# Reordering VectorE and GpSimd work around the head statistics of a self-attention block

## The chip, the cores and the metric

The kernel runs on one core of a Trainium2 chip. The metric is the time of the launch on the device in microseconds (us). Three runs are shown, and their median is used. One more execution was taken by the hardware profiler, and all views of the profile come from it.

The engines of the core are named as in the profile: PE (TensorE, matrix products and transposes), PEld (its weight loads), DVE (VectorE), ACT (ScalarE), POOL (GpSimd) and SP (SyncE, which only issues transfers here). Each engine works through its own queue of instructions in order; between engines they wait on semaphores.

## The reference, cut to what matters

The program is two layers of a gated transformer over 16 batch items of 128 tokens and 256 features. The change touches only the first attention layer (the functions `_ln`, `_div_clamp_fp8` and `_gqa` of the reference):

```python
ln_out = _ln(hidden_states, ln_w, ln_b)
q = _fp8_linear_pertensor(ln_out, wq, wq_scale, q_in_scale).reshape(b, s, g, hpg, d)
q = _ln(q, qln_w, qln_b)
k = _fp8_linear_pertensor(ln_out, wk, wk_scale, k_in_scale).reshape(b, s, g, d)
k = _ln(k, kln_w, kln_b)
v = _fp8_linear_pertensor(ln_out, wv, wv_scale, v_in_scale).reshape(b, s, g, d)
core = _gqa(q, k, v).reshape(b, s, nh * d)          # self-attention, 16 heads, 8 groups, d = 128
qx = _fp8_linear_pertensor(ln_out, wqx, wqx_scale, qx_in_scale)  # cross-attention to the context
...
xout = _gqa(qx, kx, vx).reshape(b, s, nh * d)
catq = _div_clamp_fp8(jnp.concatenate([core, xout], axis=-1), proj_smooth)
return jnp.einsum('bsi,oi->bso', catq, wproj) * (proj_in_scale * proj_w_scale)
```

Here `_ln` normalises each head over its 128 features, `_fp8_linear_pertensor` divides its input by a scale per feature, clamps it, rounds it to 8-bit floating point and multiplies by a weight matrix, and `_gqa` is softmax attention in which two query heads share one key head. After this layer come a gated feed-forward layer, a second attention layer and a layer of eight experts; the change does not touch them.

## The kernel before

The first attention layer is 32 units of work (class `Unit`): one self-attention unit for each batch item (units 0 to 15), then one cross-attention unit for each (16 to 31). A unit takes four steps of the loop over `n` at the end of the class, and in each step several units are at different stages. In the loop, `do(n, lag, name)` calls a stage for one of a unit's four chunks of four heads, and `once(n, step, name)` calls a stage once for a unit.

The stages, in the order in which a self-attention unit meets them:

- `prep_norm`, `prep_tr`, `prep_scale`: the item's rows are normalised (DVE), transposed (PE) and divided by the scales of the four kinds of input, queries, keys, values and cross queries (POOL, tile `in_y`).
- `prep_round` and `prep_last`: rounding to 8 bits in `e4m3`. Four DVE operations (clamp, mask of the exponent, scaling it, an addition, lines 225 to 231) give the tiles `e_e` and `e_t`; POOL subtracts them (line 237). Before the change it writes two tiles, `xs` (queries, keys and values, 768 columns) and `xx` (cross queries, 256 columns). SP then stores `xx` in DRAM (line 409), from where the cross unit loads it 16 units later.
- `project` and `evict`: eight blocks of 512 columns, two for the keys, four for the queries, two for the values, as products on PE (line 431), copied to `raw` or `vt` by ACT (lines 443 and 440). `bn` takes the statistics of each head of `raw` on DVE (line 452).
- `rstd`: four small DVE operations on 24 columns (lines 459 to 464, `q_dif` and `q_var`) give the variances of the unit's 24 heads; `rsqrt0` gives their inverse roots: logarithm and exponential on ACT (lines 308 and 309), then one Newton step of three DVE operations (lines 310 to 312, `q_r`).
- `mult`: POOL scales four heads of `raw` by `q_r` (line 475, six times a unit). `heads`: PE transposes them (line 486), and ACT evicts them with weight and bias of the norm into `kT` or `qT` (line 495).
- `scores` (PE, line 504), `top` (the maximum, DVE, line 512), `exp` (ACT, line 520), `recip` (DVE, line 528), `divide` (POOL, line 532), `probs` (transposes on PE, line 540, evicted by ACT, line 542), `values` (PE, line 550), `smooth` (DVE, line 561).
- `quant` and `quant_last`: the same rounding for the attention's output; POOL writes `cat` (line 237). `output` multiplies by the projection (PE, line 591), and `residual` adds the result to the input (DVE, line 605).

In the step in which `rstd` of unit u runs, unit u-1 is at its chunk 2: its scores, maximum and exponentials come first in the loop. The same step has `prep_last` of unit u+1, the `mult` of the two key blocks and of the first query block of unit u, and `quant` of the last chunks of unit u-2. In the next step the keys of unit u+1 are projected, and the division of chunk 2 of unit u-1 comes.

The order on each engine is not the order of the program's text. A scheduler arranges the instructions of each engine when the kernel is built: an instruction that is ready by the scheduler's own estimate of times is placed, and among several ready ones that which comes first in the text. The queue that results is fixed, and on the chip each engine keeps to it. `stay_after(ins, other)` adds an edge for this arrangement: `ins` is put behind `other`. Both are on the same engine in all uses here, so it costs no wait. Before the change it is used only in `quant_last`, where the last write of `cat` is put behind the third scaling of the unit that is two ahead (`scaled`).

Tiles rotate: `raw` has nine buffers, most others two, `in_y` one. In PSUM the scores have two buffers, which the estimate in `rsqrt0` shares, and the values one.

Of the kernel before, what the change touches and what calls it, by code (L numbers as in the profile page):

```python
# [18 lines left out]
P = 128  # L19
B = 16  # L20
# [15 lines left out]
def flamingo_kernel(  # L36
# [182 lines left out]
    def e4m3(dsts, y, pool):  # L219


        n = y.shape[1]
        e = pool.tile([P, n], BF16, tag="e8_e", name="e8_e")
        t = pool.tile([P, n], BF16, tag="e8_t", name="e8_t")
        nc.vector.tensor_scalar(y, y, FP8_MAX, -FP8_MAX, ALU.min, ALU.max)
        nc.vector.tensor_scalar(
            e.bitcast(U16), y.bitcast(U16), 0x7F80, None, ALU.bitwise_and
        )

        nc.vector.tensor_scalar(e, e, 2.0**-6, 24.0, ALU.max, ALU.mult)  # L230
        nc.vector.tensor_tensor(t, y, e, ALU.add)  # L231

        def last(other=None):
            at = 0
            for dst in dsts:
                part = slice(at, at + dst.shape[1])
                ins = nc.gpsimd.tensor_tensor(dst, t[:, part], e[:, part], ALU.subtract)  # L237
                if other is not None:
                    stay_after(ins, other)
                at += dst.shape[1]  # L240

        return last
# [11 lines left out]
    with (  # L254
# [48 lines left out]
        def rsqrt0(v, n, tag):  # L303

            a = small.tile([P, n], F32, tag=f"{tag}_a", name=f"{tag}_a", bufs=2)
            r = small.tile([P, n], F32, tag=f"{tag}_r", name=f"{tag}_r", bufs=2)
            est = ps_sc([P, n])
            nc.scalar.activation(a, v, AF.Ln)
            nc.scalar.activation(est, a, AF.Exp, scale=-0.5)
            nc.vector.scalar_tensor_tensor(a, est, -0.5, v, ALU.mult, ALU.mult)  # L310
            nc.vector.tensor_tensor(a, est, a, ALU.mult)
            nc.vector.scalar_tensor_tensor(r, a, 1.5, est, ALU.add, ALU.mult)  # L312
            return r

        norms = {}

        def stats(g):
# [13 lines left out]
            rr = rsqrt0(v, 4, "x")  # L331
# [3 lines left out]
        class Unit:  # L335
# [61 lines left out]
            def prep_round(self):  # L397
                if self.cross:
                    return
                xs = ap.tile([P, 6 * P], F32R, tag="xs", name="xs")  # L400
                xx = ap.tile([P, KD * P], F32R, tag="xx", name="xx")
                self.last = e4m3([xs, xx], self.y.rearrange("p i t -> p (i t)"), ap)
                self.xs, self.xx = xs, xx

            def prep_last(self):
                if self.cross:
                    return
                self.last()
                nc.sync.dma_start(out=xqx[self.b], in_=self.xx.bitcast(F32))
                lhs = [  # L410
                    [self.xs[:, (2 * kind + k) * P : (2 * kind + k + 1) * P] for k in range(KD)]
                    for kind in range(3)
                ]
                self.q_lhs, self.k_lhs, self.v_lhs = lhs[K_Q], lhs[K_K], lhs[K_V]

# [38 lines left out]
            def rstd(self):  # L454
# [4 lines left out]
                nc.vector.tensor_tensor(dif, st[:, :, 1], st[:, :, 4], ALU.subtract)  # L459
# [4 lines left out]
                nc.vector.scalar_tensor_tensor(var, var, 1.0 / P, dif, ALU.mult, ALU.add)  # L464
                self.r = rsqrt0(var, 24, "q")
# [44 lines left out]
            def top(self, c):  # L510
                mx = small.tile([P, 4], F32, tag="mx", name="mx")
                nc.vector.tensor_reduce(mx, self.sc[c], AX.X, ALU.max, negate=True)  # L512
# [17 lines left out]
            def divide(self, c):  # L530
                e, sums = self.e[c]
                nc.gpsimd.tensor_tensor(  # L532
                    e, e, sums[:, :, None].to_broadcast([P, 4, P]), ALU.mult
                )

# [30 lines left out]
            def quant(self, c):  # L566
                if c % 2 == 0:
# [4 lines left out]
                    self.cy.rearrange("p h s -> p (h s)"), ap,  # L572
# [119 lines left out]
        for n in range(first, last + 1):  # L692
# [12 lines left out]
            do(n, 0, "top")  # L705
            do(n, 0, "exp")
            if ab[0]:
                ab[0][0].project(ab[0][1])
                ab[0][0].evict(ab[0][1])
            once(n, -6, "prep_last")  # L710
# [4 lines left out]
            once(n, -2, "rstd")  # L715
# [5 lines left out]
            do(n, 3, "quant")  # L721
# [13 lines left out]
            once(n, -7, "prep_round")  # L735
# [618 lines left out]
```

## Time and profile before

| | |
|---|---|
| median of three runs | 1501.8 us (1501.51, 1501.80, 1504.62) |
| the profiled execution's own time | 1503.01 us |
| its span from first to last instruction | 1501.3 us |
| busy share PE, PEld, DVE, ACT, POOL | 91%, 64%, 66%, 56%, 46% |
| mean granted PE clock | 0.966 of full |
| instructions | 21652 |
| PE busy from 40 to 440 us (self-attention) | 361.23 of 400 us |
| PE busy from 440 to 870 us (cross-attention) | 415.93 of 430 us |

The page gives averages over stages with different limits, so the shares alone say little. Lines of the trace name an engine, a line of the program, an operation, the tiles written and read (`out<-in`), and the shape. In the timeline the first two numbers are the start and the duration in us, and the bracket gives how long the engine stood idle before, and what it then waited for. Where several instructions of one kind follow each other, they are one row (x3), and the duration is that of the row. Self-attention blocks in the steady part last 26.5 us, or 27.5 to 28 us in some of them.

### The profile page before, as it was taken

To read this page: it belongs to the slowest core of one execution; us is meant where nothing else is said; L and a number is where in the kernel's file an instruction comes from. 1 tells how busy PE (TensorE), PEld (TensorE's weight loads), DVE (VectorE), ACT (ScalarE), POOL (GpSimd) and SP (SyncE) were. 2 spreads that over 40 slices of the span, in tenths; PEclk is the share of its full clock that TensorE was granted. 3 is DMA by queue.
4 is the path that set the end of the run, shared out by engine and by line. 5 is a ranking of instruction groups with operands and counts; after the bars stand their busy time and mean duration, and the time that the engine had idled before them with its cause. 6 is when DMAs were issued, how large, how long until landed. Compare 5 with 4: busy or idle time off the path is not lost. (4 is left out here: it accounts for less than half of the span.)

```text
span 1501.3 us, 21652 instructions
## 1 busy us (share of the span) xinstructions
PE 1369.6 (91%) x6852; PEld 964.4 (64%) x6852; DVE 988.6 (66%) x2597; ACT 838.4 (56%) x2496; POOL 687.6 (46%) x615
## 2 busy tenths in 40 slices
PE   2789899899988999999999997999999999985998
PEld 1578778687776777777777766555544444444887
DVE  7867878778689777777676764453478787762100
ACT  3666566666656676666666663164476575741221
POOL 4476677677766565656556563121032322111111
PEclk9699999999999999999999998899999999986999
DMA  4300101000013100000000000700042212122652
GB/s 133 110 17 23 38 22 38 21 22 27 22 55 104 45 29 19 15 16 17 12 18 15 15 4 27 211 8 14 31 128 53 75 50 63 40 75 76 196 189 70
DMA packets 78770, 80.37 MB, mean 54 GB/s; under 512 B 15291, under 2 KB 64891, under 8 KB 78656
## 3 DMA queue, kind: packets, MB, share of 16 engines
q1 hardware_dynamic: 65152, 55.29, 12.7%
q10 hardware_dynamic: 11456, 17.63, 3.6%
q0 software_dynamic: 2048, 6.07, 1.1%
q8 instruction: 55, 0.90, 0.3%
q14 instruction: 59, 0.48, 0.1%
HBM read 57.14 MB, written 22.05 MB: 53 GB/s over the span
## 5 line engine op out<-in xcount | busy, mean ns | idle before, releaser
L532 POOL TENSOR_TENSOR e<-e,sums 128x512 f32<-128x512 f32 x128 | 141.4, 1105 | 239.7 <-DVE sums L528 100.8
L475 POOL TENSOR_TENSOR raw<-raw,q_r 128x512 f32<-128x512 f32 x192 | 211.3, 1126 | 21.0 <-DVE q_r L312 19.6
L520 ACT ACTIVATE e<-ps_sc,mx 128x128 f32<-128x128 f32 x512 | 181.1, 368 | 63.6 <-DVE mx L512 58.1
L452 DVE BATCH_NORM_STATS2 q_st<-raw 128x6 f32<-128x128 f32 x768 | 174.2, 279 | 64.2 <-ACT raw L443 63.6
L591 PE MATMUL ps_acc<-wp,cat 128*128 128x512 f32 x512 | 159.3, 433 | 14.0 <-POOL cat L237 13.4
L504 PE MATMUL ps_sc<-kT,qT 128*128 128x128 f32 x1024 | 140.9, 281 | 23.9 <-ACT qT L495 23.9
L542 ACT COPY eT<-ps_tr 128x512 f32<-128x512 f32 x128 | 75.3, 588 | 156.3 <-PE ps_tr L540 156.3
L504 PEld LDWEIGHTS ps_sc<-kT,qT 128*128 128x128 f32 x1024 | 132.4, 194 | 44.1 <-ACT qT L495 36.6
L237 POOL TENSOR_TENSOR cat<-e_t,e_e 128x1024 fp32r<-128x1024 bf16 x64 | 136.6, 2135 | 43.5 <-DVE e_t L231 43.5
L1082 ACT ACTIVATE e<-ps_sc,mx 128x128 f32<-128x128 f32 x512 | 139.0, 392 | 30.5 <-DVE mx L1073 30.1
L550 PE MATMUL ps_pv<-eT,vt 128*128 128x256 f32 x512 | 133.8, 383 | 1.0 <-DVE cat_y L561 1.0
L443 ACT COPY raw<-ps_mm 128x512 f32<-128x512 f32 x192 | 113.8, 593 | 29.2 <-PE ps_mm L431 25.8
L591 PEld LDWEIGHTS ps_acc<-wp,cat 128*128 128x128 f32 x512 | 94.6, 191 | 53.4 <-POOL cat L237 20.1
L486 PE MATMUL ps_tr<-ident,raw 128*128 128x128 f32 x768 | 115.2, 276 | 13.6 <-POOL raw L475 11.6
L486 PEld LDWEIGHTS ps_tr<-ident,raw 128*128 128x128 f32 x768 | 91.6, 141 | 47.5 <-POOL raw L475 20.5
L561 DVE TENSOR_TENSOR cat_y<-ps_pv,r_sm 128x512 bf16<-128x512 f32 x128 | 87.1, 680 | 47.2 <-PE ps_pv L550 46.7
L550 PEld LDWEIGHTS ps_pv<-eT,vt 128*128 128x128 f32 x512 | 97.3, 192 | 30.9 <-issue 10.5
L512 DVE TENSOR_REDUCE mx<-ps_sc 128x4 f32<-128x512 f32 x128 | 87.2, 682 | 38.5 <-PE ps_sc L504 37.8
L495 ACT ACTIVATE qT<-ps_tr,hv 128x512 f32<-128x512 f32 x128 | 101.2, 791 | 19.9 <-PE ps_tr L486 17.7
L520 ACT ACTIVATION_READ_ACCUMULATOR e<-ps_sc,mx 128x1 f32 x512 | 105.4, 206 | 0.0
L1093 PEld LDWEIGHTS ps_tr<-ident,e 128*128 128x128 f32 x512 | 59.9, 142 | 64.9 <-ACT e L1082 28.1
L1073 DVE TENSOR_REDUCE mx<-ps_sc 128x8 f32<-128x1024 f32 x64 | 77.6, 1212 | 30.2 <-PE ps_sc L1066 20.9
(221 smaller groups left out, 2687.0 us busy)
## 6 DMA issues: line engine op xcount, KB each, us to landing
w1t<-in_w ACTq DMA_DIRECT2D x8, 1024.0 KB
w2t<-in_w ACTq DMA_DIRECT2D x8, 1024.0 KB
disp<-empty SPq DMA_DIRECT2D x16, 257.0 KB
xe<-disp SPq DMA_DIRECT2D x8, 514.0 KB
ctx<-in_ctxT SPq DMA_DIRECT2D x32, 128.0 KB
stage<-in_wprojT SPq DMA_DIRECT2D x16, 256.0 KB
ods<-og SPq DMA_DIRECT2D x128, 32.0 KB
ov<-ods SPq DMA_DIRECT2D x32, 128.0 KB
```

What stands on the lines that cost most here:

```text
L237: ins = nc.gpsimd.tensor_tensor(dst, t[:, part], e[:, part], ALU.subtract)
L443: nc.scalar.copy(raw.rearrange("p h d -> p (h d)"), pm)
L452: nc.vector.bn_stats(self.st[:, 4 * blk + j, :], self.raws[blk][:, j, :])
L475: ins = nc.gpsimd.tensor_tensor(src, src, self.r[:, 4 * blk : 4 * blk + 4, None].to_broadcast([P, 4, P]), ALU.mult,)
L486: nc.tensor.transpose(pt[:, j, :], src[:, j, :], ident)
L495: nc.scalar.activation(dst, pt, AF.Identity, scale=hv[:, col : col + 1], bias=hv[:, col + 1 : col + 2])
L504: nc.tensor.matmul(pscore[:, j, :], qT[:, j, :], self.kT[:, 2 * c + j // 2, :], start=True, stop=True,)
L520: nc.scalar.activation(e[:, j, :], pscore[:, j, :], AF.Exp, bias=self.mx[:, j : j + 1], accum_out=sums[:, j : j + 1],)
L532: nc.gpsimd.tensor_tensor(e, e, sums[:, :, None].to_broadcast([P, 4, P]), ALU.mult)
L550: nc.tensor.matmul(pv[:, 2 * g : 2 * g + 2, :], self.vt[:, gg * P : (gg + 1) * P], eT[:, 2 * g : 2 * g + 2, :], start=True, stop=True,)
L591: nc.tensor.matmul(self.acc, self.cat[c // 2][:, h % 8, :], wpr[self.cross, c][:, j, :, :], start=(h == 0), stop=(h == 15),)
L1082: nc.scalar.activation(e[:, i, :], s[:, i // NQ, i % NQ, :], AF.Exp, bias=mx[:, i : i + 1])
```

## The change

Four things are changed, all in the first attention layer.

1. On DVE, in the step of `rstd`: first the maximum of the scores (`top`), then the variances (`rstd`, moved up in the text, its first operation put behind the maximum), then the rounding of the next unit's inputs (`prep_round`, moved from the end of the step before to this step; its clamp is put behind the last operation of the variances, or behind the maximum where there are no variances). The clamp of `quant` in this step is put behind the last operation of the Newton step.
2. The rounded inputs are four tiles of 256 columns instead of two of 768 and 256. `prep_last` now writes only that of the keys.
3. `prep_rest` is new: POOL writes the tiles of the queries, values and cross queries, behind the third scaling of the unit before, and SP stores the cross queries' tile after that.
4. The division of chunk 2 of a self-attention unit is put behind the third scaling of the unit after it.

```diff
@@ -216,13 +216,15 @@
             mean[:, :, None].to_broadcast([P, nh, P]), ALU.subtract,
         )
 
-    def e4m3(dsts, y, pool):
+    def e4m3(dsts, y, pool, behind=None):
 
 
         n = y.shape[1]
         e = pool.tile([P, n], BF16, tag="e8_e", name="e8_e")
         t = pool.tile([P, n], BF16, tag="e8_t", name="e8_t")
-        nc.vector.tensor_scalar(y, y, FP8_MAX, -FP8_MAX, ALU.min, ALU.max)
+        ins = nc.vector.tensor_scalar(y, y, FP8_MAX, -FP8_MAX, ALU.min, ALU.max)
+        if behind is not None:
+            stay_after(ins, behind)
         nc.vector.tensor_scalar(
             e.bitcast(U16), y.bitcast(U16), 0x7F80, None, ALU.bitwise_and
         )
@@ -230,14 +232,13 @@
         nc.vector.tensor_scalar(e, e, 2.0**-6, 24.0, ALU.max, ALU.mult)
         nc.vector.tensor_tensor(t, y, e, ALU.add)
 
-        def last(other=None):
-            at = 0
-            for dst in dsts:
-                part = slice(at, at + dst.shape[1])
-                ins = nc.gpsimd.tensor_tensor(dst, t[:, part], e[:, part], ALU.subtract)
+        def last(other=None, which=range(len(dsts))):
+            for i in which:
+                at = sum(d.shape[1] for d in dsts[:i])
+                part = slice(at, at + dsts[i].shape[1])
+                ins = nc.gpsimd.tensor_tensor(dsts[i], t[:, part], e[:, part], ALU.subtract)
                 if other is not None:
                     stay_after(ins, other)
-                at += dst.shape[1]
 
         return last
 
@@ -309,9 +310,11 @@
             nc.scalar.activation(est, a, AF.Exp, scale=-0.5)
             nc.vector.scalar_tensor_tensor(a, est, -0.5, v, ALU.mult, ALU.mult)
             nc.vector.tensor_tensor(a, est, a, ALU.mult)
-            nc.vector.scalar_tensor_tensor(r, a, 1.5, est, ALU.add, ALU.mult)
-            return r
-
+            return r, nc.vector.scalar_tensor_tensor(r, a, 1.5, est, ALU.add, ALU.mult)
+
+        tops = {}
+        vars_ = {}
+        rstds = {}
         norms = {}
 
         def stats(g):
@@ -328,7 +331,7 @@
 
             v = small.tile([P, 4], F32, tag="v1", name="v1", bufs=1)
             nc.vector.tensor_scalar(v, mv[:, :, 1], 1.0 + EPS, EPS * EPS, ALU.mult, ALU.add)
-            rr = rsqrt0(v, 4, "x")
+            rr, _ = rsqrt0(v, 4, "x")
             for j in range(4):
                 norms[4 * g + j] = (xg[:, j, :], mv[:, j, 0:1], rr[:, j : j + 1])
 
@@ -394,24 +397,35 @@
                 )
                 self.y = y
 
-            def prep_round(self):
+            def prep_round(self, n):
                 if self.cross:
                     return
-                xs = ap.tile([P, 6 * P], F32R, tag="xs", name="xs")
-                xx = ap.tile([P, KD * P], F32R, tag="xx", name="xx")
-                self.last = e4m3([xs, xx], self.y.rearrange("p i t -> p (i t)"), ap)
-                self.xs, self.xx = xs, xx
+                kinds = [
+                    ap.tile([P, KD * P], F32R, tag=f"x{slot}", name=f"x{slot}")
+                    for slot in ("qs", "ks", "vs", "x")
+                ]
+                self.last = e4m3(
+                    kinds, self.y.rearrange("p i t -> p (i t)"), ap, vars_.get(n, tops.get(n))
+                )
+                self.xs, self.xx = kinds[:3], kinds[3]
 
             def prep_last(self):
                 if self.cross:
                     return
-                self.last()
-                nc.sync.dma_start(out=xqx[self.b], in_=self.xx.bitcast(F32))
+                self.last(which=[K_K])
                 lhs = [
-                    [self.xs[:, (2 * kind + k) * P : (2 * kind + k + 1) * P] for k in range(KD)]
+                    [self.xs[kind][:, k * P : (k + 1) * P] for k in range(KD)]
                     for kind in range(3)
                 ]
                 self.q_lhs, self.k_lhs, self.v_lhs = lhs[K_Q], lhs[K_K], lhs[K_V]
+
+            def prep_rest(self):
+
+                if self.cross:
+                    return
+                u = units.index(self) - 1
+                self.last(units[u].scaled if u >= 0 else None, [K_Q, K_V, 3])
+                nc.sync.dma_start(out=xqx[self.b], in_=self.xx.bitcast(F32))
 
 
             def project(self, blk):
@@ -451,18 +465,22 @@
                 for j in range(4):
                     nc.vector.bn_stats(self.st[:, 4 * blk + j, :], self.raws[blk][:, j, :])
 
-            def rstd(self):
+            def rstd(self, n):
 
                 st = self.st
                 var = small.tile([P, 24], F32, tag="q_var", name="q_var", bufs=1)
                 dif = small.tile([P, 24], F32, tag="q_dif", name="q_dif", bufs=1)
-                nc.vector.tensor_tensor(dif, st[:, :, 1], st[:, :, 4], ALU.subtract)
+                ins = nc.vector.tensor_tensor(dif, st[:, :, 1], st[:, :, 4], ALU.subtract)
+                if n in tops:
+                    stay_after(ins, tops[n])
                 nc.vector.scalar_tensor_tensor(dif, dif, 0.25, dif, ALU.mult, ALU.mult)
                 nc.vector.scalar_tensor_tensor(
                     var, st[:, :, 2], P * EPS, st[:, :, 5], ALU.add, ALU.add
                 )
-                nc.vector.scalar_tensor_tensor(var, var, 1.0 / P, dif, ALU.mult, ALU.add)
-                self.r = rsqrt0(var, 24, "q")
+                vars_[n] = nc.vector.scalar_tensor_tensor(
+                    var, var, 1.0 / P, dif, ALU.mult, ALU.add
+                )
+                self.r, rstds[n] = rsqrt0(var, 24, "q")
 
             def mult_q(self, c):
                 self.mult(c + 2)
@@ -507,9 +525,9 @@
                     )
                 self.sc[c] = pscore
 
-            def top(self, c):
+            def top(self, c, n):
                 mx = small.tile([P, 4], F32, tag="mx", name="mx")
-                nc.vector.tensor_reduce(mx, self.sc[c], AX.X, ALU.max, negate=True)
+                tops[n] = nc.vector.tensor_reduce(mx, self.sc[c], AX.X, ALU.max, negate=True)
                 self.mx = mx
 
             def exp(self, c):
@@ -529,9 +547,12 @@
 
             def divide(self, c):
                 e, sums = self.e[c]
-                nc.gpsimd.tensor_tensor(
+                ins = nc.gpsimd.tensor_tensor(
                     e, e, sums[:, :, None].to_broadcast([P, 4, P]), ALU.mult
                 )
+                u = units.index(self) + 1
+                if c == 2 and u < B:
+                    stay_after(ins, units[u].scaled)
 
             def probs(self, c):
                 e, _ = self.e.pop(c)
@@ -563,13 +584,13 @@
                     r_sm[:, h0 : h0 + 4, None].to_broadcast([P, 4, P]), ALU.mult,
                 )
 
-            def quant(self, c):
+            def quant(self, c, n):
                 if c % 2 == 0:
                     return
                 cat = ap.tile([P, 8, P], F32R, tag="cat", name="cat")
                 self.clast = e4m3(
                     [cat.rearrange("p h s -> p (h s)")],
-                    self.cy.rearrange("p h s -> p (h s)"), ap,
+                    self.cy.rearrange("p h s -> p (h s)"), ap, rstds.get(n),
                 )
                 self.cat[c // 2] = cat
 
@@ -702,23 +723,25 @@
             do(n, 1, "divide")
             do(n, 0, "scores")
             do(n, 2, "probs")
-            do(n, 0, "top")
+            do(n, 0, "top", n)
             do(n, 0, "exp")
             if ab[0]:
                 ab[0][0].project(ab[0][1])
                 ab[0][0].evict(ab[0][1])
+            once(n, -2, "rstd", n)
+            once(n, -6, "prep_round", n)
             once(n, -6, "prep_last")
             do(n, 3, "values")
             do(n, 3, "smooth")
             if ab[0]:
                 ab[0][0].bn(ab[0][1])
-            once(n, -2, "rstd")
             for blk in range(2):
                 once(n, -2, "mult", blk)
                 once(n, -1, "heads", blk)
             do(n, -2, "mult_q")
             do(n, -1, "heads_q")
-            do(n, 3, "quant")
+            once(n, -6, "prep_rest")
+            do(n, 3, "quant", n)
             if ab[1]:
                 ab[1][0].project(ab[1][1])
                 ab[1][0].evict(ab[1][1])
@@ -732,7 +755,6 @@
             once(n, -8, "prep_norm")
             once(n, -8, "prep_tr")
             once(n, -7, "prep_scale")
-            once(n, -7, "prep_round")
 
     G = 4
     NT = G * P
```

## The prediction

> **What bounds the kernel now.** I read the page's first two parts first. TensorE (PE) is busy in 91% of the span, so the kernel can only gain where PE stands idle, or where its work shrinks; the change touches no PE work. Then I cut the span into stretches and compared a steady self-attention block with a steady cross-attention block (columns: stretch, us, then busy us and instructions for PE, PE's weight loads, VectorE, ScalarE, GpSimd, then granted clock):
>
> ```profile
> PE 1369.6 (91%) x6852; PEld 964.4 (64%) x6852; DVE 988.6 (66%) x2597; ACT 838.4 (56%) x2496; POOL 687.6 (46%) x615
> ...
> 310.00:336.50 26.50, 24.70 (x148) 20.76 (x147) 20.00 (x61) 17.11 (x54) 19.01 (x16) 1.00 0.08 23
> ...
> 600.00:626.50 26.50, 26.32 (x138) 19.64 (x137) 19.22 (x56) 17.12 (x53) 15.39 (x12) 1.00 0.05 15
> ```
>
> The clock is full in both. The cross block leaves PE 0.18 us idle, the self block 1.80 us of 26.50. Next, who PE waits for between 50 and 440 us (total, times, longest):
>
> ```profile
> PE ps_sc L504 <- ACT qT L495: 18.5, 12, 1.7
> PE ps_tr L486 <- POOL raw L475: 10.9, 21, 2.0
> ...
> PE ps_mm L431 <- DVE q_dif L459: 1.1, 1, 1.1
> ```
>
> Twelve blocks lose 1.46 to 1.69 us each at the scores, and 0.34 to 1.4 us at the transposes of the scaled heads. Last, the timeline of one such block shows why:
>
> ```profile
> 316.91 1.65 POOL L237 TENSOR_TENSOR xs<-e_t,e_e 128x768 fp32r<-128x768 bf16 x1 [0.63 <-DVE e_t L231]
> 317.36 1.26 DVE L459 TENSOR_TENSOR q_dif<-q_st 128x24 f32<-128x24 f32 x1
> ...
> 319.68 0.17 DVE L464 SCALAR_TENSOR_TENSOR q_var<-q_var,q_dif 128x24 f32<-128x24 f32 x1
> ...
> 319.89 0.22 ACT L308 ACTIVATE q_a<-q_var 128x24 f32<-128x24 f32 x1 [0.85 <-DVE q_var L464]
> 320.02 0.76 ACT L495 ACTIVATE qT<-ps_tr,hv 128x512 f32<-128x512 f32 x1
> ...
> 320.83 1.16 PE L504 MATMUL ps_sc<-kT,qT 128*128 128x128 f32 x8 [1.46 <-ACT qT L495]
> ...
> 322.27 3.03 POOL L475 TENSOR_TENSOR raw<-raw,q_r 128x512 f32<-128x512 f32 x3
> ...
> 324.36 0.66 PE L486 MATMUL ps_tr<-ident,raw 128*128 128x128 f32 x4 [0.34 <-POOL raw L475]
> ...
> 325.26 2.13 POOL L237 TENSOR_TENSOR cat<-e_t,e_e 128x1024 fp32r<-128x1024 bf16 x1
> ```
>
> A 24-column subtraction (q_dif, median 0.20 us over the kernel) takes 1.26 us and ends 0.06 us after GpSimd's write of xs. The logarithm on ScalarE waits for its result, the eviction of qT is queued behind the logarithm, and PE's scores wait for qT. The scaling of the heads then starts at 322.27, and PE meets it at 324.36. I use this block's times below.
>
> **What the change removes.** VectorE now takes the maximum, then the variances, then the rounding of the inputs. The scores end at 314.14. With the last 0.86 us of statistics ahead of it, the maximum (0.68) ends at 315.7, where it ended at 317.44. The variances' four operations (0.20, 0.17, 0.19, 0.17, some overlapped: 0.7) end near 316.4, not 319.85; GpSimd has no xs to write then. The exponentials on ScalarE (four at a pitch of 0.345) run 315.7 to 317.2, the value copy 0.6, logarithm 0.22, qT 0.76: qT is ready by 318.6. PE comes free for the scores at 318.89, after the transposes that start at 318.53. So the 1.46 us wait goes. Exponential and Newton steps follow, so q_r is ready near 319.4 instead of 321.93, and the heads' wait goes if GpSimd keeps up. Summed: scores 18.5; heads' waits in the same twelve blocks 10.9 less 2.35 (the block near 105 us) and 0.34 (near 80) = 8.2; the block near 100 us, 1.05 + 2.35 = 3.4. That is 30.1 us over 13 blocks, and no more is to be had in them.
>
> **What it adds and moves.** The rounding's four VectorE operations (0.43, 0.42, 0.43, 0.75, with a smoothing of 0.68 likely between) start at 316.4 and end near 319.05. GpSimd then writes the keys' inputs. The row for a 256-column write is 0.67 us (xx), so 319.75. The keys' projection can start when the scores leave PE, 318.89 + 0.9 = 319.8: no wait, with 0.05 us to spare. If q_r comes first and one scaling is ahead, 1 us.
>
> Behind it on GpSimd stand three scalings, then queries', values' and cross inputs (3 x 0.67), then cat (2.13), then the division of chunk 2 (1.04), which is now held behind the scalings as well. The input writes come to 4 x 0.67 = 2.68 us instead of 1.65 + 0.67 = 2.32. The DMA of the cross inputs moves with its write; SP's queue has nothing behind it that PE reads, and the data is read back sixteen blocks later. The rounding of cat is held behind the Newton steps on VectorE, so its four operations now lie beside the scalings, as they do in a cross block:
>
> ```profile
> 627.72 6.00 POOL L475 TENSOR_TENSOR raw<-raw,q_r 128x512 f32<-128x512 f32 x5
> ...
> 628.05 1.14 DVE L226 TENSOR_SCALAR e_e<-cat_y 128x1024 uint16<-128x1024 uint16 x1
> 629.23 1.15 DVE L230 TENSOR_SCALAR e_e<-e_e 128x1024 bf16<-128x1024 bf16 x1
> 630.41 1.41 DVE L231 TENSOR_TENSOR e_t<-cat_y,e_e 128x1024 bf16<-128x1024 bf16 x1
> ```
>
> There five scalings took 6.00 us, against 1.03 each alone: 0.17 us more apiece, and the VectorE operations 1.14 to 1.41 instead of about 0.43 to 0.69. The Trainium skill ("SBUF — State Buffer", section "Who interferes with whom") has a rule that speaks against this placing: a VectorE operation in a two-port mode, or with two SBUF inputs, and a GpSimd operation exclude each other, and whoever issues second is blocked for the other's whole instruction. By the rule three scalings could each lose a whole VectorE operation, 0.43 to 0.69, some 1.5 us a block; by the row they lose 0.5. I take the row. With the rule the gain would be 13 us smaller.
>
> So GpSimd: keys' inputs to 319.75, scalings at a pitch of 1.2 to 323.3, the rest to 325.4, cat to 327.5, division to 328.6. The heads' transposes (PE there about 1.5 us earlier than before, 321.9) need the first two scalings at 320.95 and 322.15: I charge 0.3 us a block, bounds 0 and 0.7. The projection with cat began at 327.45 and, 1.8 us earlier, would begin at 325.65: cat is 1.85 us late for it. PE has the next scores (0.9), a query projection (1.0) and values (0.9) to put first, if its queue is ordered so; the transposes that wait for the division (329.38 before, 327.6 then) can also stand behind these. Bounds 0 (all covered) and 1.85 plus something at the division; I take a third, 0.6. Together 0.9 x 13 = 11.7 us given back.
>
> Costed at nothing: in the 16 cross blocks the maximum goes ahead of the subtraction (623.90 and 623.78 now, 0.1 us), and cat's rounding already followed the Newton steps (627.47, 627.59). If the smoothing slips behind those steps, its cover is the next values, 5 us later (632.57); without it, 0.6 us a block. The boundary at 440 to 475 us, with 2.43 and 3.32 us waits, may shift by 2 us either way; I take 0. At the start, unit 0's rounding is issued after half of the queries' weights: between -1.4 us (0.67 instead of 2.08 before PE's first projection at 26.54) and +6; PE then waits 3.10 us for weights at 38.61, which covers most. I take 0. Unit 1's rounding now comes after unit 0's variances, which ended at 51.85, while its xs write ended at 50.6: K inputs up to 54.6 with 2.0 + 0.67, 4 us later, less what the variances gain (1.6 us of L460 was spent beside that write). I take +1.5, bounds 0 and 4.
>
> **Sum**: -30.1 + 11.7 + 1.5 = -16.9 against the profiled execution's own 1503.0 (span 1501.3): 1486.1. The median of the runs is 1.2 lower: 1485.
>
> **Rivals.**
> - *All of it is gained.* PE saturates as in the cross blocks (0.18 us idle): -30 + 1.5, 1473. For it: PE has other work at each late place. Against: GpSimd's queue is longer and nearer. Chance 0.2.
> - *GpSimd becomes the bound (slower).* One mechanism: cat stands behind the three input writes, and PE's queue keeps the projection where it was. Break-even is cat ending at 327.45, the old start. There a block lasts what it does now, and each further tenth of a us costs 1.3 us over 13 blocks. If scalings and writes lose what the rule says (1.0 more), cat ends at 328.5, 1.05 past that point: +13.7 us, less a third for blocks where PE has other work, so +9 on 1501.8, near 1510. For it: my cat time is 327.5, on the edge. Against: PE's weight loads wait little for cat now (0.8 us in 12 blocks), and 2.8 us of other PE work is at hand. Chance 0.22.
> - *The wait changes its name.* stay_after orders one engine; PE's queue had one keys' matmul ahead of the scores, at 318.89. If all four stay there, PE waits for the keys' inputs until 319.75 and the scores start at 320.8, as before; only heads' waits go, about 0.3 us a block: 1498, between 1494 and 1503. Chance 0.13.
> - *The forecast*, 1485, between 1477 and 1496: 0.45.
>
> **How the numbers follow.** A measurement of this kernel tells about 0.2% (3 us) from no change, so faster means under 1498.8 and slower over 1504.8. Faster: forecast and full gain 0.65, and a third of the renamed wait, 0.04: 0.69. Same: the rest of it near 1500, 0.06. Slower: 0.25, of which 0.22 the GpSimd case. The range 1472 to 1507 leaves out a little of the full gain and the further part of the slower case, together under 0.2.
>
> **What would show it.** Right: in the timeline q_dif takes 0.2 us and comes after the maximum and before in_y's clamp; the wait of L504 for qT falls from 18.5 to under 3 us; scalings start about 2.5 us earlier relative to the scores; self blocks last 25.0 to 25.6 us. Wrong: PE's waits list shows L591 for cat, L540 for e or L431 for the keys' inputs with more than 1 us a block, or blocks of 26.5 us and more; or the first 82 us have grown by more than 4.

## The result: 3.4% slower, and the profile after

The changed kernel takes 1555.1 us (median of 4 runs, 1550.1 to 1556.0); the kernel before took 1501.7 on the same chip. The ratio on record is 1.0335, with a 95% interval of 1.0313 to 1.0357 (the two medians alone give 1.0355). The profiled execution took 1555.4 us with a span of 1553.7, so 52.4 us more than the span before.

The first part of the page after, PE's row:

```profile
PE 1386.7 (89%) x6852; PEld 981.2 (63%) x6852; DVE 992.4 (64%) x2597; ACT 839.5 (54%) x2496; POOL 701.5 (45%) x647
```

PE runs the same 6852 instructions, yet is busy 17.1 us longer, and its share fell from 91% to 89%. Two things must have happened: new idle time, and slower work. The waits of PE between 50 and 440 us of the kernel after (total, times, longest) give the first:

```profile
PE ps_acc L612 <- POOL cat L239: 41.3, 12, 6.4
PE ps_tr L504 <- ACT kT L513: 7.1, 9, 0.8
PE ps_mm L445 <- POOL xks L239: 3.3, 3, 1.9
PE ps_tr L504 <- POOL raw L493: 3.2, 5, 2.1
```

The wait of the scores for qT, 18.5 us before, is off the list, and the wait for scaled heads fell from 10.9 to 3.2. A wait that was nowhere near the top before, that of the output projection (L612) for cat, stands at 41.3 us. Before, cat was ready only just in time: its write ended at 327.39 in the block of the prediction, and the projection began at 327.45 without a wait:

```profile
327.45 1.20 PE L591 MATMUL ps_acc<-wp,cat 128*128 128x512 f32 x4
```

The stretches of the kernel after give the second. The columns are those of the prediction's second fence; the first row is a whole self-attention block, the second the 6 us that begin 0.5 us before the projection starts:

```profile
317.70:347.70 30.00, 26.18 (x148) 22.11 (x147) 22.36 (x65) 17.24 (x56) 19.84 (x17) 0.94 0.07 20
...
328.00:334.00 6.00, 5.52 (x23) 4.91 (x24) 1.27 (x2) 2.13 (x10) 3.47 (x4) 0.72 0.01 3
```

The block has the 148 PE instructions that it had before, and lasts 30.00 us instead of 26.50. PE is busy 26.18 us instead of 24.70: 1.48 us more for the same work. Behind the wait the granted clock is 0.72 over 6 us; from 334 us to 347 us, in the rest of the block, it is 1.00 again. PE's timeline in this block shows both at the place:

```profile
324.82 0.66 PE L665 MATMUL ps_mm<-av,ctx 128*128 128x64 f32 x4
...
328.48 1.20 PE L612 MATMUL ps_acc<-wp,cat 128*128 128x512 f32 x4 [3.00 <-POOL cat L239]
329.51 1.46 PE L522 MATMUL ps_sc<-kT,qT 128*128 128x128 f32 x8
...
331.48 2.05 PE L445 MATMUL ps_mm<-wq,xqs 128*128 128x512 f32 x4
```

The last matmuls of kv1 (L661 and L665, products of the context that a later layer reads) end at 325.48, the projection starts at 328.48. The scores behind it take 1.46 us, where those at full clock take 1.05 to 1.16, and a query projection 2.05, where it took 1.18 before. Who wrote cat, and when, is in GpSimd's timeline of the same block:

```profile
317.81 0.67 POOL L239 TENSOR_TENSOR xks<-e_t,e_e 128x256 fp32r<-128x256 bf16 x1 [3.58 <-DVE e_t L233]
318.44 3.58 POOL L493 TENSOR_TENSOR raw<-raw,q_r 128x512 f32<-128x512 f32 x3
321.99 1.11 POOL L239 TENSOR_TENSOR xqs<-e_t,e_e 128x256 fp32r<-128x256 bf16 x1
323.06 0.67 POOL L239 TENSOR_TENSOR xvs<-e_t,e_e 128x256 fp32r<-128x256 bf16 x1
323.69 0.67 POOL L239 TENSOR_TENSOR xx<-e_t,e_e 128x256 fp32r<-128x256 bf16 x1
324.32 1.04 POOL L550 TENSOR_TENSOR e<-e,sums 128x512 f32<-128x512 f32 x1
325.32 1.03 POOL L493 TENSOR_TENSOR raw<-raw,q_r 128x512 f32<-128x512 f32 x1
326.32 2.11 POOL L239 TENSOR_TENSOR cat<-e_t,e_e 128x1024 fp32r<-128x1024 bf16 x1
```

VectorE's part of cat's rounding (e_t) ends at 322.57 and the third scaling at 322.02:

```profile
321.16 1.41 DVE L233 TENSOR_TENSOR e_t<-cat_y,e_e 128x1024 bf16<-128x1024 bf16 x1
```

GpSimd then runs three input writes, a division and a fourth scaling, and takes cat only at 326.32. The engine is not idle from 317.8 until cat is written, but its order is not PE's: what PE needs next is at the end of the row.

In two of the twelve blocks the scheduler put three scalings there instead of one. From GpSimd's and PE's timelines at that place:

```profile
292.63 3.03 POOL L493 TENSOR_TENSOR raw<-raw,q_r 128x512 f32<-128x512 f32 x3
295.62 2.11 POOL L239 TENSOR_TENSOR cat<-e_t,e_e 128x1024 fp32r<-128x1024 bf16 x1
...
297.79 2.07 PE L612 MATMUL ps_acc<-wp,cat 128*128 128x512 f32 x4 [6.38 <-POOL cat L239]
```

The projection alone then takes 2.07 us, where it takes 1.1 to 1.2 at the full clock. In the 6 us from 297.80 the granted clock is 0.59.

**Where the 52.4 us are.** I timed the blocks by the start of kv1 (L640 before, L661 after), which comes once a block. The first of the marks used stands at 108.93 before and 107.36 after, the mark twelve blocks later at 434.10 and 474.86. So the part ahead of the marks is 1.6 us shorter, and the twelve blocks are 42.3 us longer: 27.1 us each before and 30.6 after. The last 11.6 us come at the passage to cross-attention and in its first units; from 860 us (after: 912 us) on the distance stays. The stretches between the marks, before and after, in the columns of above, and PE's wait for cat in the second:

```profile
108.93:434.10 325.17, 298.23 (x1754) 249.60 (x1753) 251.20 (x744) 205.70 (x652) 225.74 (x181) 1.00 0.09 29
...
107.36:474.86 367.50, 315.30 (x1754) 266.15 (x1753) 252.09 (x743) 206.15 (x653) 237.89 (x205) 0.93 0.08 24
...
PE ps_acc L612 <- POOL cat L239: 42.8, 12, 6.4
```

At the same 1754 instructions PE is busy 17.1 us longer, at a granted clock of 0.93 instead of 1.00. Its idle time has grown by 25.3 us: 42.8 for cat (ten waits of 3.0 us, two of 6.4) and 8.3 for kT come in, the 18.5 for qT and some 8 for the heads go.

### The profile page after: what moved, and what is told of

Same layout as the page of the kernel before. It is cut to its first block, busy times and chain, and to the rows that moved or that the text cites. A ratio compares the mean times of both kernels' runs of the same rounds, so it can differ in the third digit from the quotient of the medians.

```text
span 1553.7 us, 21692 instructions
## 1 busy us (share of the span) xinstructions
PE 1386.7 (89%) x6852; PEld 981.2 (63%) x6852; DVE 992.4 (64%) x2597; ACT 839.5 (54%) x2496; POOL 701.5 (45%) x647
## 5 line engine op out<-in xcount | busy, mean ns | idle before, releaser
L550 POOL TENSOR_TENSOR e<-e,sums 128x512 f32<-128x512 f32 x128 | 136.3, 1065 | 245.2 <-ACT raw L457 131.2
L493 POOL TENSOR_TENSOR raw<-raw,q_r 128x512 f32<-128x512 f32 x192 | 220.8, 1173 | 12.8 <-DVE q_r L313 11.4
L612 PE MATMUL ps_acc<-wp,cat 128*128 128x512 f32 x512 | 166.2, 449 | 64.7 <-POOL cat L239 62.9
L612 PEld LDWEIGHTS ps_acc<-wp,cat 128*128 128x128 f32 x512 | 98.0, 198 | 107.0 <-POOL cat L239 70.8
L522 PEld LDWEIGHTS ps_sc<-kT,qT 128*128 128x128 f32 x1024 | 141.6, 205 | 23.3 <-ACT qT L513 14.4
L522 PE MATMUL ps_sc<-kT,qT 128*128 128x128 f32 x1024 | 148.8, 292 | 2.5 <-ACT qT L513 2.5
L504 PEld LDWEIGHTS ps_tr<-ident,raw 128*128 128x128 f32 x768 | 92.9, 143 | 52.6 <-issue 27.1
```

The lines of the kernel that those rows point to most:

```text
L493: ins = nc.gpsimd.tensor_tensor(src, src, self.r[:, 4 * blk : 4 * blk + 4, None].to_broadcast([P, 4, P]), ALU.mult,)
L504: nc.tensor.transpose(pt[:, j, :], src[:, j, :], ident)
L522: nc.tensor.matmul(pscore[:, j, :], qT[:, j, :], self.kT[:, 2 * c + j // 2, :], start=True, stop=True,)
L550: ins = nc.gpsimd.tensor_tensor(e, e, sums[:, :, None].to_broadcast([P, 4, P]), ALU.mult)
L612: nc.tensor.matmul(self.acc, self.cat[c // 2][:, h % 8, :], wpr[self.cross, c][:, j, :, :], start=(h == 0), stop=(h == 15),)
```

## The experiments

Unless said otherwise a diff is against the kernel after, the ratio is to the kernel before on the same chip (medians 1501.1, 1502.2 and 1503.7 in the three groups) with its 95% interval, and a block's length is taken between kv1 marks; where one figure is given, it is that of most blocks. In the expectations, theory A says that cat is late because of what stands ahead of it in GpSimd's queue while PE's queue keeps the projection where it is.

**1. Cat ahead of the three input writes (e1_cat_first).** The write of cat is kept as `wrote`; the input writes, the division and the later scalings are held behind it. Everything that the change does on VectorE stays.

```
-  self.last(units[u].scaled if u >= 0 else None, [K_Q, K_V, 3])
+  first = units[u - 2].wrote if u >= 2 else units[u].scaled if u >= 0 else None
+  self.last(first, [K_Q, K_V, 3])
...
+  elif blk > 2 and 2 <= u < B:
+      stay_after(ins, units[u - 2].wrote)
...
-      stay_after(ins, units[u].scaled)
+      stay_after(ins, units[u - 2].wrote if u >= 2 else units[u].scaled)
...
-  self.clast(units[b].scaled if b < NU else None)
+  self.wrote = self.clast(units[b].scaled if b < NU else None)
...
+  once(n, -5, "prep_rest")     # behind quant_last
   ...
-  once(n, -6, "prep_rest")
```

> Changed kernel, but GpSimd writes cat of the last chunks directly behind the third scaling; the three input writes, the division of chunk 2 and the scalings 4 to 6 stand behind that write. Theory A (cat is late because of what GpSimd does ahead of it: three input writes, a division and a scaling, 4.3 us, and PE keeps the projection in its place): cat is written from about 0.5 us after the third scaling and ends before PE is there; the wait for cat falls from 3.0 us a block to under 0.3, the PE clock stays full, self blocks last about 25.5 us, and the time is about 1490 us. Theory B (cat is late because its rounding on VectorE, now behind the Newton steps and beside the scalings, ends too late): GpSimd would stand idle until e_t is there, PE would still wait 2 us or more, and the time would be 1535 us or more.

Measured: 1494.9 us, 0.9950 (0.9934 to 0.9966); a block lasts 25.9 us. GpSimd's timeline and PE's, and PE's waits between 50 and 440 us:

```profile
310.04 3.58 POOL L495 TENSOR_TENSOR raw<-raw,q_r 128x512 f32<-128x512 f32 x3
314.31 2.13 POOL L239 TENSOR_TENSOR cat<-e_t,e_e 128x1024 fp32r<-128x1024 bf16 x1 [0.69 <-DVE e_t L233]
...
316.88 1.17 PE L617 MATMUL ps_acc<-wp,cat 128*128 128x512 f32 x4
...
PE ps_tr L566 <- POOL e L555: 6.9, 14, 0.8
...
PE ps_acc L617 <- POOL cat L239: 3.0, 3, 1.5
```

GpSimd even stands idle for 0.69 us until cat's rounding is ready, and the kernel is still 60 us faster than the changed one: the order was the harm, not the amount of GpSimd's work. The division (L555) is late instead, 0.5 us a block, as one expects where it is pushed back by a write of 2.1 us.

**2. Without the hold of cat's rounding (e2_no_round_edge).** Cat's rounding on VectorE no longer has to follow the Newton steps.

```
-  self.cy.rearrange("p h s -> p (h s)"), ap, rstds.get(n),
+  self.cy.rearrange("p h s -> p (h s)"), ap,
```

> Changed kernel without one edge: the rounding of cat is no longer held behind the Newton steps on VectorE; the scheduler then puts cat on GpSimd behind three scalings and three input writes, ahead of the division and the fourth scaling. Theory A (GpSimd's queue): two operations of 1.04 us fewer stand ahead of cat, so PE's wait falls from 3.0 to about 1.0 us a block and the clock recovers; about 1508 us. Theory B (rounding on VectorE too late): the wait falls to nothing; about 1490 us.

Measured: 1505.6 us, 1.0028 (1.0018 to 1.0038); a block lasts 26.8 us. PE's waits between 50 and 440 us, then GpSimd's timeline, then PE's at two blocks:

```profile
PE ps_acc L612 <- POOL cat L239: 24.2, 14, 1.8
...
324.85 0.66 POOL L239 TENSOR_TENSOR xx<-e_t,e_e 128x256 fp32r<-128x256 bf16 x1
325.48 2.11 POOL L239 TENSOR_TENSOR cat<-e_t,e_e 128x1024 fp32r<-128x1024 bf16 x1
327.55 1.04 POOL L550 TENSOR_TENSOR e<-e,sums 128x512 f32<-128x512 f32 x1
...
327.64 1.20 PE L612 MATMUL ps_acc<-wp,cat 128*128 128x512 f32 x4 [1.75 <-POOL cat L239]
...
354.48 2.08 PE L612 MATMUL ps_acc<-wp,cat 128*128 128x512 f32 x4 [1.75 <-POOL cat L239]
```

With that one edge gone the build-time scheduler puts cat directly behind the three writes, ahead of division and scaling. So an order given to VectorE decided the order on GpSimd. The likely reason, which no run tests, is that in the scheduler's estimate the hold makes cat's rounding late, and that it fills GpSimd's queue with what it believes to be ready sooner. What is left is the wait behind the three writes, about 1.7 us a block, and the kernel is back near the time before. The last two rows are two blocks with the same wait: in the first the projection takes 1.20 us behind it, in the second 2.08. Behind 4 of the 13 such waits from 100 us on the clock fell (0.76 or 0.77 over 7 us), behind the other 9 it stayed at 1.00.

**3 and 5. Work for PE in the gap (e3_filler, e5_filler_six).** If a wait lowers the clock, PE work that nobody reads, put into the wait, must make the kernel faster. Behind kv1's matmuls come 10 (e3) or 6 (e5) more products of 128x256, into columns that are not read.

```
+  for i in range(FILL):
+      nc.tensor.matmul(pm[:, 2 * P :], cx[:, i % KD, :], cx, start=True, stop=True)
```

> Changed kernel with ten more products of 128x256 on PE in each self block, between kv1 and the projection that waits for cat; they write unused columns and are read by nobody. They are about 2.4 us of work in the 3.0 us wait. Theory C (the wait costs twice: PE's clock is lowered after it, and the products after the wait run slower): the granted clock is back at 1.00 in the self blocks, the products after the wait take what they took before, blocks fall from 30.0 to about 28.5 us and the time to about 1535 us, although PE does more. Rival (the slower products have another reason, or the clock does not depend on the wait): no gain, 1555 us or more.

> As the run with ten additional products on PE between kv1 and the projection, but with six: those ten took 4.2 us and overshot the wait, these should take 2.5 us in the 3.0 us. Theory C (the wait for cat also lowers PE's clock, which makes the products behind it slower by about 1.5 us a block): the granted clock stays near 1.00 in the self blocks and a block falls from 30.0 to about 28.5 us, the time to about 1538 us. Rival (the clock has nothing to do with this wait): no block is shorter, 1555 us.

Measured for ten: 1560.7 us, 1.0385 (1.0363 to 1.0407), a block 29.6 us. The products took 4.2 us, more than the gap of 3.0. The total is that of the rival, 1555 us or more, but with this overshoot it does not decide on the clock. With six (each is two instructions in the trace, x12), from PE's timeline and stretches:

```profile
318.41 2.81 PE L672 MATMUL ps_mm<-ctx 128*128 128x256 f32 x12
321.58 1.20 PE L612 MATMUL ps_acc<-wp,cat 128*128 128x512 f32 x4 [0.36 <-POOL cat L239]
322.61 1.05 PE L522 MATMUL ps_sc<-kT,qT 128*128 128x128 f32 x8
...
321.50:327.50 6.00, 5.92 (x34) 5.18 (x35) 3.14 (x11) 3.48 (x15) 3.12 (x4) 1.00 0.14 36
```

Measured: 1547.0 us, 1.0299 (1.0278 to 1.0319). Cat is as late as before, PE has more to do, and the kernel is 8 us faster than the changed one (1544.6 to 1549.9 against 1550.1 to 1556.0; the intervals of the two ratios just overlap). The block is the clearer sign: the clock behind the wait is 1.00, the scores are back to 1.05 us, and it is 28.48 us long instead of 30.00. These 1.5 us are the price of the lowered clock, the same 1.48 that PE's busy time had shown. The total fell by less than I had expected for two reasons: the blocks with three scalings ahead of cat still waited 3.7 us and ran slow behind it, and of the 15.0 us gained by the last mark (459.82 instead of 474.86) 7 were lost again behind it: the marks of the last two kv1, which have the additional products too, lie 6.5 us further apart than in the changed kernel.

**4. VectorE's order alone (e4_vector_only).** GpSimd writes xs and xx in two pieces at once, as in the kernel before, and the division is not held; maximum, variances and roundings keep the new order on VectorE.

```
-  kinds = [ap.tile([P, KD * P], F32R, tag=f"x{slot}", ...) for slot in ("qs", "ks", "vs", "x")]
+  xs = ap.tile([P, 6 * P], F32R, tag="xs", name="xs")
+  xx = ap.tile([P, KD * P], F32R, tag="xx", name="xx")
...
-  self.last(which=[K_K])
+  self.last()
...
-  if c == 2 and u < B:
-      stay_after(ins, units[u].scaled)
...
-  once(n, -6, "prep_rest")
```

> Only VectorE's order is changed (maximum, variances, rounding of the inputs, cat's rounding behind the Newton steps); GpSimd writes the inputs as before in two tiles, at once, and the division is not held. The scheduler then places xs, xx, six scalings and cat in this order. Theory A (GpSimd's queue ahead of cat): cat ends about 12 us after the first input write, so PE waits some 3.7 us or more and the time is 1555 to 1575 us. Rival (the splitting and deferring of the input writes does the harm): the wait for cat is gone and the time is 1480 to 1495 us.

Measured: 1570.1 us, 1.0446 (1.0420 to 1.0473), blocks of 31.3 to 33.0 us. PE's waits between 50 and 440 us, and GpSimd's timeline:

```profile
PE ps_acc L609 <- POOL cat L239: 35.4, 12, 3.5
PE ps_mm L444 <- POOL xs L239: 18.1, 13, 2.5
...
330.35 6.66 POOL L492 TENSOR_TENSOR raw<-raw,q_r 128x512 f32<-128x512 f32 x6
336.97 2.11 POOL L239 TENSOR_TENSOR cat<-e_t,e_e 128x1024 fp32r<-128x1024 bf16 x1
```

Here six scalings stand ahead of cat, and the keys' projection has a wait of its own for xs. The new order on VectorE alone is worse than the whole change: splitting the inputs' write and holding the division gave some 15 us back.

**6. Cat early, by both means (e6_cat_early).** The hold of experiment 2 is gone, and the input writes stand behind cat as in experiment 1 (the later scalings and the division are not held behind it).

> Changed kernel with two edits: the rounding of cat is not held behind the Newton steps, and the three late input writes stand behind the write of cat. Theory A: with cat directly behind the third scaling and e_t early, PE's wait for cat is gone, GpSimd does not idle ahead of cat, the wait for kT (0.82 us a block) shrinks; blocks of about 25.3 us, time about 1487 us. Theory B (the early rounding of cat delays the scalings[...] by as much as it gains): no better than 1495 us.

Measured: 1489.6 us, 0.9917 (0.9901 to 0.9933), a block 26.0 us. PE waits 1.5 us in all for cat; the largest waits are now the division's (11.2 us, 14 times) and the scaled heads' (6.8 us, 15 times).

**7. The old order with the split alone (e7_before_split).** Against the kernel before: four tiles, the keys' inputs written at once, the other three behind cat; VectorE's and PE's order stay.

```
-  self.last = e4m3([xs, xx], self.y.rearrange("p i t -> p (i t)"), ap)
+  self.last = e4m3(kinds, self.y.rearrange("p i t -> p (i t)"), ap)
...
-  self.last()
+  self.last(which=[K_K])
...
+  once(n, -5, "prep_rest")     # behind cat's write
```

> The kernel before with one edit: the rounded inputs are four tiles, GpSimd writes only the keys' tile where it wrote xs and xx, and the other three behind cat. VectorE's and PE's orders are those of before. Theory D (the bubble of before comes from the subtraction q_dif, held up while GpSimd writes xs): q_dif falls from 1.26 us to 0.3 to 0.5, PE's wait for qT from 1.46 to about 0.5 us, the scalings start about 1 us earlier; blocks of about 25.3 us, 1486 us. Rival (q_dif is slow for another reason, or qT is late anyway): unchanged, 1500 us or more.

Measured: 1487.7 us, 0.9906 (0.9890 to 0.9923), a block 25.5 us. VectorE's and PE's timelines:

```profile
306.79 0.28 DVE L468 TENSOR_TENSOR q_dif<-q_st 128x24 f32<-128x24 f32 x1
...
309.30 1.16 PE L513 MATMUL ps_sc<-kT,qT 128*128 128x128 f32 x8 [0.50 <-ACT qT L504]
```

The stall of q_dif, which started all this, does not need another order on VectorE. With only 0.67 us of GpSimd's write beside it, it takes 0.28 us instead of 1.26, and the scores wait 0.50 us instead of 1.46.

**8. PE's projection one step later (e8_output_later).** GpSimd and VectorE are as in the kernel after; PE takes the output projection, and what follows it, one chunk later.

```
-  first, last = -11, 4 * NU + 7
+  first, last = -11, 4 * NU + 8
...
-  do(n, 5, "output")
-  once(n, 8, "residual")
+  do(n, 6, "output")
+  once(n, 9, "residual")
```

> Changed kernel with the projection that uses cat, and the residual behind it, one step of the loop later. GpSimd's order up to cat and VectorE's are those of the changed kernel, so cat is just as late; PE's projection with it stands some 5 us later in PE's queue, behind the scores, transposes, a query projection and values. Theory A (the harm is that PE's fixed queue has this projection ahead of work that is ready): the wait for cat and the low clock are gone, blocks of about 25.5 us, time about 1490 us. Rival (GpSimd is the bound of the block): PE waits as long at another place, 1530 us or more.

Measured: 1483.7 us, 0.9881 (0.9866 to 0.9896), blocks of 25.5 to 26.6 us: the lowest median of all, though its interval just overlaps that of experiment 7. GpSimd's timeline, PE's, and PE's longest wait between 50 and 440 us:

```profile
317.16 1.03 POOL L493 TENSOR_TENSOR raw<-raw,q_r 128x512 f32<-128x512 f32 x1
318.16 2.13 POOL L239 TENSOR_TENSOR cat<-e_t,e_e 128x1024 fp32r<-128x1024 bf16 x1
...
316.13 1.17 PE L612 MATMUL ps_acc<-wp,cat 128*128 128x512 f32 x4
...
321.64 1.10 PE L612 MATMUL ps_acc<-wp,cat 128*128 128x512 f32 x4
...
PE ps_sc L522 <- ACT qT L513: 19.2, 13, 5.0
```

Cat is still behind a division and a fourth scaling and ends at 320.29. The projection at 316.13 reads the cat before it, and the one that reads this cat starts at 321.64, with 1.35 us to spare. So GpSimd was not the bound: it had time for all of the work, and with another place for the projection in PE's queue the same cat is in time. The scores have a wait for qT again, 0.4 to 1.6 us in most blocks, and what else limits this version was not followed.

**9 and 10. Two repairs together (e9_early_later, e10_split_later).** Experiment 9 is 6 with the later output of 8; experiment 10 is 7 with it.

> Both repairs of the changed kernel together: cat directly behind the third scaling with its rounding not held, and the projection one loop step later. If PE's wait for cat was the only harm, either repair was enough and both together bring little over the better one: 1480 to 1485 us. If the waits left in the single repairs (0.8 us for the division in one, about 1 us for qT in the other) are each cured by the other, 1470 to 1478 us.

> The kernel before with two edits: the split input writes, the late three behind cat, and the projection one loop step later. VectorE's order is that of before. Waits left with the first edit alone are 0.5 us for qT and 0.3 us for the scaled heads a block, none for cat; a later projection cures neither, so 1485 to 1490 us. If the projection's place also frees GpSimd's order, up to 10 us less.

Measured: 1493.9 us, 0.9946 (0.9932 to 0.9959), with blocks of 26.7 us, and 1498.3 us, 0.9962 (0.9949 to 0.9974), with blocks of 26.8. Both are misses: each is slower than either of its parts. Between 50 and 440 us PE waits 13.0 us for divisions in the ninth (13 times), and 22.1 us for qT in the tenth (24 times).

Every edge and every moved step is a new input to the scheduler, which then writes out all five queues anew. Which of its estimates makes these two worse than their parts was not found out, and stays open.

## Why the prediction was wrong

- **The stall that the change removes: right.** The prediction said that q_dif would fall from 1.26 to 0.2 us and that the wait for qT would go. VectorE's timeline after, one block:

```profile
344.07 0.67 DVE L530 TENSOR_REDUCE mx<-ps_sc 128x4 f32<-128x512 f32 x1
344.66 0.19 DVE L473 TENSOR_TENSOR q_dif<-q_st 128x24 f32<-128x24 f32 x1
345.20 0.42 DVE L225 TENSOR_SCALAR in_y<-in_y 128x1024 bf16<-128x1024 bf16 x1
```

  Maximum, variances, clamp, in this order, and 0.19 us. The scores' waits for qT are 2.5 us in the whole kernel. Experiment 7 shows the cause as the prediction had it: less of GpSimd's write beside q_dif, and most of the stall is gone with no new order.
- **Start and keys' inputs: right in the main.** PE's scores at 85.08 us before start at 85.31 after: the start cost some 0.2 us, less than the 1.5 taken and inside the bounds of 0 and 4. The keys' projection waits for its inputs 3 times between 50 and 440 us, 3.3 us in all. The rival in which the scores wait as long as before did not come.
- **The scalings' pitch: right, and the row rather than the rule.** Three scalings beside cat's rounding take 3.58 us, 1.19 each (1.2 predicted), against 3.03 for three alone, so they lose 0.18 each. The whole-instruction block of the Trainium skill ("SBUF — State Buffer", "Who interferes with whom") would have been about 0.5 each by the prediction's estimate. Most of the price falls on VectorE instead: its two operations on 1024 columns that took 0.43 and 0.69 us before take 1.15 and 1.41, which fits the rule for whoever comes second. I had taken e_t to be ready in time all the same, and it was.
- **The wrong step: when cat comes, and what PE does meanwhile.** The prediction let cat follow the input writes, "cat to 327.5, division to 328.6". GpSimd's queue has the division and a scaling first. Relative to the input writes that is 2.0 us later, and 4.0 in the two blocks with three scalings. Then it said of PE that it "has the next scores (0.9), a query projection (1.0) and values (0.9) to put first, if its queue is ordered so", and charged "a third, 0.6". The queue is not ordered so: the projection stands directly behind kv1, as before. The true term is 3.00 us in a plain block and 6.4 in one with three scalings ahead of cat. Its upper bound, 1.85 plus something, did not hold either, since it took GpSimd's order as fixed by the source.
- **The missing term: the clock.** The sum had no price for what an idle PE does to the work behind it. It is 1.48 us in this block by PE's busy time, 1.5 by experiment 5, and 17.1 us over the twelve blocks.
- **The sum of a block, corrected.** 26.50 us, less the idle 1.80, plus 3.82 of new idle (3.00 for cat and 0.82 at the keys' transposes, where PE, early now, waits for the eviction to kT), plus 1.48 for the clock: 30.00, as measured. Without the wait for cat and its clock it would be 25.52, inside the 25.0 to 25.6 that the prediction gave; experiment 8, where this wait is gone and one for qT is back, has blocks of 25.5 to 26.6.
- **The passage to cross-attention: missed.** It was put at 0, with 2 us either way, and cost 11.6. Between the last mark and 621 us (after: 673 us) PE waits 8.5 us for cat and 5.8 for kT, where it was 3.3 and 1.2, and is busy 2.9 us longer. What sets the order there was not followed.
- **The slower rival had the mechanism.** "Cat stands behind the three input writes, and PE's queue keeps the projection where it was" is what happened. At 1510 its price was too small by 45 us, as it had neither the division and scaling ahead of cat, nor the clock, nor the passage. Experiment 2, in which only the three writes stand ahead, is close to that rival as it was worked out: 1505.6.

## What to carry to other kernels

When a stall is removed upstream, ask for each engine which instruction its queue holds next and whether its input has moved as well: PE's queue had 2.8 us of other work at hand and stood idle 3.0, because that work stood behind the projection. Where a scheduler writes the queues, an edge on one engine can re-order another, so cost the order after the change and not the old one with edits. A wait of PE can have a second price behind it, the clock: look for it in busy time that grows at the same count of instructions.

## What the runs showed of the hardware

- The clock behind a wait of PE. This is the granted clock of the 7 us behind each wait for cat (before: for qT) between 100 and 440 us:

| kernel | waits, us each | clock fell behind | granted over 7 us there |
|---|---|---|---|
| before | 1.46 to 1.69 | 0 of 12 | - |
| experiment 2 | 1.66 to 1.76 | 4 of 13 | 0.76 to 0.77 |
| after, plain blocks | 3.0 | 7 of 9 | 0.60 to 0.76 |
| experiment 4 | 3.0 to 3.5 | 11 of 11 | 0.56 to 0.78 |
| after, three scalings ahead of cat | 6.4 | 2 of 2 | 0.62 to 0.65 |

  Equal waits do not cost the same, and there is no single length from which on the clock falls. What decides, for the most part, can be read from the same traces. The granted clock changes only at marks 3.41 us apart, and it falls to 0.50 for one such stretch or several. Cut along these marks, experiment 2's wait that ends at 327.64 and the equal one that ends at 354.48 look like this:

```profile
323.56:326.97 3.41, 2.33 (x16) 1.66 (x14) 0.87 (x4) 2.39 (x6) 3.41 (x5) 1.00 0.14 43
326.97:330.39 3.42, 2.75 (x18) 2.52 (x19) 0.62 (x1) 0.18 (x1) 3.42 (x4) 1.00 0.21 58
...
350.87:354.28 3.41, 1.86 (x14) 1.29 (x11) 0.87 (x4) 1.92 (x5) 3.41 (x4) 1.00 0.19 58
354.28:357.69 3.41, 3.21 (x11) 2.83 (x12) 0.00 (x0) 0.00 (x0) 3.41 (x5) 0.50 0.14 38
```

  The first wait is shared by two stretches, with PE busy 2.33 and 2.75 us in them. The second falls almost whole into one, which is left with 1.86 us, and the next runs at half. In all twelve traces, between 100 and 440 us, PE was busy 56% at most in each of the 33 full-clock stretches that a drop followed, and 46% at least in the others; in between it went either way (PE's busy time is modelled in part). So the place of a wait among these marks counts beside its length. The Trainium skill ("TensorE: Matmul & The Clock Gate") asks in "HAM oscillation — how this bites in real kernels" for no idle gaps over about 3.4 us; here 1.75 us could be enough, and 3.0 mostly was. In "What's actually happening" it has the activity watched in windows of about 3.4 us that run freely; the marks agree with that. One stretch at half is 1.7 us lost, or 0.76 over 7 us, which is what most of the rows show.
- More work on PE made the kernel faster: 6 products in the gap, a row of 2.8 us, and a block of 28.48 us instead of 30.00 (experiment 5).
- A VectorE subtraction of 24 columns took 1.26 us beside a GpSimd write of 768 columns, 0.28 beside one of 256, and 0.19 with none.
